# A graph network layer on one core: another order of the end, 28 row tiles instead of 26, and four row addresses with one register load

## The chip, the cores and the metric

The kernel runs on one core of one Trainium2 chip. A core has TensorE (PE: matmuls, with its weight loads shown as PEld), VectorE (DVE), ScalarE (ACT), GpSimd (POOL) and SyncE (SP), which compute or issue in their own order and wait for each other by semaphores. The metric is device time in microseconds (us), the median of several runs.

## The reference

There are 6250 nodes with 128 features, and 206,250 edges sorted by receiver. For each edge, two small networks give a weight vector of 128; the query of the receiver, the key of the sender and this weight are multiplied, summed over each of 8 heads, scaled, and multiply the sender's value. The results are summed by receiver, added to the node features, and normalized by row.

```python
w_ij = silu(edge_feats @ rad_W1 + rad_b1) @ rad_W2 + rad_b2
w_ij = w_ij + (silu(chi_scalar @ sph_W1 + sph_b1) @ sph_W2 + sph_b2)
q_i = (node_feats @ Wq).reshape(-1, 8, 16)[receivers]
k_j = (node_feats @ Wk).reshape(-1, 8, 16)[senders]
alpha = (q_i * w_ij * k_j).sum(axis=-1) / sqrt(16) * cutoffs[:, None]
v_j = (node_feats @ Wv)[senders].reshape(-1, 8, 16)
out = segment_sum(alpha[..., None] * v_j, receivers) / 16
x = layernorm(node_feats + out.reshape(-1, 128))
```

## The kernel before

A tile is 128 edges, one per partition. Four tiles are a quad (512 edges), four quads a group. There are 403 quads in 101 groups; the last group, 100, has three. Inside a group the quads are taken in the order 0, 2, 1, 3; `order` is the list of all quads in that order, and a place in it is called a position.

First the kernel makes a table `kv_tab` in device memory with key and value of every node. Quads at the first ten positions get their sender rows from x instead. For every later quad, POOL gathers four tiles of `kv_tab` rows by sender index (`gathers`, issued 14 positions ahead, at line 127 of the helper `gather`), with 16 buffers. Receivers are sorted, so the receivers of a quad lie in a window of 32 nodes and those of a group in a window of 128; one-hot tables turn queries into rows per edge (`hotT`, `one_hots_T`) and sum messages by receiver (`hot`, `one_hots`).

**Row tiles.** At 26 positions, spread over positions 20 to 392, the last tile of the quad is not gathered by POOL (`row_quads`). SP copies its 128 rows instead, each with a DMA of 1 KB whose source address stands in a register (`load_rows`, lines 150 to 168). It does so in four parts, at four slots before the quad's turn: one register load of 32 addresses from `at_i` (line 163) and 32 DMAs (line 167). The last part comes 8 positions before the quad, so the last of all at position 384. `multiply` and `messages` take such a quad in two instructions, one for three tiles and one for the row tile (`kv_parts`).

**The main loop** (lines 685 to 744) goes over groups g and four slots; the order of each engine is the order of the calls. In a slot, TensorE does the first layers for the quad two ahead (`first_layers`), the queries (`q_at_edges`) and the second layers (`weigh`) for the quad one ahead; ScalarE does the silus; VectorE does `multiply` (query by key, line 526) for the quad one ahead, then `scores` (lines 534, 536, 538) and `messages` (line 551) for the current quad. Messages of group g - 1 are summed in the slots of group g (`sum_quads`). Then `part_sums`, `sum_group` and `place` bring a group's sums to its 128 rows together with what the group before it left (`tot`).

SP's own work in the loop, in this order: in slot 0 `load_x` (the 128 rows of x for group g + 3: a register load of the address from `gb_i`, line 234, and a DMA, line 237); in slot 2 `load_feats` (group g + 3, line 178) and `load_rel` (the receivers `relb` for group g + 2, line 189); in every slot one `write_rows` (one group's rows of out, line 647, if any are ready), and `load_rows`. `load_x` and `load_feats` wait for a mark of TensorE, so that SP does not run ahead. VectorE reads `relb` in slot 1 of the group before (`one_hots_T`, line 218).

`statistics` (slot 3) adds x to a group's sums and takes mean and variance (`moments`, lines 613 to 616); every fourth group, four groups are normalized (`roots`, line 621, and `normalize`, lines 629 to 635).

**The end** (lines 745 to 799) is written out for the last three quads, called a, b and c, all of group 100. Their sums go straight to 128 rows (`sum_wide`, line 578). Quad c is taken in two halves, each with multiply, scores, messages and sums of its own, and groups 97, 98 and 99 are normalized one by one between these; group 100 follows, and its rows are the last write (line 799).

Of the kernel before, what the change touches and what calls it, by code (L numbers as in the profile page):

```python
# [44 lines left out]
ROW_BYTES = 2 * D * 4  # L45
XQ = 10
RING = 16
ROW_TILES = 26
ROW_FIRST = 20
ROW_LAST = 392  # L50
ROW_LEAD = 8
ROW_UNIT = 32
CHECK = 20
XL = 3
NEIGHBORS = 16.0
EPS = 1e-5
SCALE = 1.0 / (math.sqrt(HD) * NEIGHBORS)
# [3 lines left out]
def gnn_kernel(ctx, tc, x, src, dst, weight, edges, rad_W1, rad_b1, rad_W2, rad_b2,  # L61
# [169 lines left out]

    def load_x(g, mark=None):

        r_of[g] = nc.values_load(gb_i[:1, g:g + 1], engines=(SP,), min_val=0, max_val=(N - P) * D * 4,
                                 skip_runtime_bounds_check_because="the table is clamped to it")
        x_of[g] = gp.tile([P, D], F32, name="x", bufs=XL + 4)
        o = nc.sync.dma_start(x_of[g].bitcast(U8), rows_from(x, r_of[g]))
        if mark is not None:
            tc.add_manual_dep(o.ins, mark.ins.name, WAIT, reason="one signal of TensorE a quad")
# [226 lines left out]
    with tc.tile_pool(name="ps", bufs=1, space=PSUM) as pp:  # L466
# [55 lines left out]
        def multiply(q, mark=None, t=slice(0, QT)):  # L522
            if t.start == 0:
                kq_of[q] = quad_of("kq", 3)
            for u, kv in kv_parts(q, t):
                o = nc.vector.tensor_tensor(kq_of[q][:, u, :], pq_of[q][:, u, :], kv[:, :, :D],  # L526
                                            op=OP.mult)
                if mark is not None:
                    after(o, mark)
# [28 lines left out]
        def sum_quads(g, t, j=None):  # L558

            if g not in po_of:  # L560
                po_of[g] = pp.tile([P, D], F32, name="po")
            for j in range(NQ) if j is None else (j,):
                o = nc.tensor.matmul(po_of[g][j * W:(j + 1) * W, :], hot_of[g][:, j * QT + t, :],  # L563
                                     msg_of[g * NQ + j][:, t, :], start=(t == 0), stop=(t == QT - 1))
            return o
# [73 lines left out]
        def statistics(g):  # L639
            moments(g, tot_of[g])  # L640
            if g < NG - LB and first_of(g + 1) > g:
                normalize(first_of(g), g + 1, roots(first_of(g), g + 1))
# [42 lines left out]
        for g in range(NG - 1):  # L685
            for slot, j in enumerate((0, 2, 1, 3)):
                q = g * NQ + j
                i = g * NQ + slot
                turned, past, old = None, mark, marks
                if slot == 0 and g == CHECK + len(checks) + 1:  # L690
                    verdict()
                if slot == 0:
                    turned = turn_q(g + 1, pp.tile([P, EQ], F32, name="pq", bufs=2))
                if slot == 1 and 2 <= g:
                    turned = sum_group(g - 2)
                if slot == 2:
                    turned = make_q(g + 1, pp.tile([P, EQ], F32, name="pq", bufs=2))
                if 1 <= g:
                    for t in ((), (0, 1), (2,), (3,))[slot]:
                        mark = sum_quads(g - 1, t)  # L700
                first_layers(order[i + 2])
                mark = q_at_edges(order[i + 1])
                marks = weigh(order[i + 1])
                silus(order[i + 2], mark, marks)
                if turned:
                    turned()
                if 1 <= g and slot == 3:
                    part_sums(g - 1)
                if i + AHEAD < len(order):
                    gathers(order[i + AHEAD], old[-QT:])  # L710
                multiply(order[i + 1], mark)
                messages(q, scores(q, marks=marks), marks=marks)
                if slot == 0:
                    if g + XL < NG:
                        load_x(g + XL, past)
                if slot == 2:
                    if g + 3 < NG:
                        load_feats(g + 3, past)
                    if g + 2 < NG:
                        load_rel(g + 2)  # L720
                if slot == 1:
                    one_hots_T(g + 1)
                    if g + 2 < NG:
                        pick(g + 2)
                    if 1 <= g:
                        place(g - 1)
                write_rows()
                load_rows(i)
                if slot == 3:
                    if 2 <= g:  # L730
                        statistics(g - 2)
                    if g + 1 < NG - 1:
                        one_hots(g + 1)
                    if CHECK <= g < CHECK + len(checks):
                        checks[g - CHECK]()
                if g == NG - 3 and slot in (0, 2):
                    wide_one_hots(order[slot // 2 - 3])
                if g == NG - 2 and slot == 0:
                    wide_one_hots(order[-1])
                    n = nc.values_load(general, min_val=0, max_val=1)  # L740
                if g == NG - 2 and slot == 2:
                    place(NG - 1)
                if g == NG - 2 and slot == 3:
                    place(g)
        g, (a, b, c) = NG - 1, order[-3:]
        halves = (slice(0, QT // 2), slice(QT // 2, QT))
# [1 line left out]
        mark = q_at_edges(b)  # L748
        marks = weigh(b)
        turned = sum_group(g - 2)  # L750
        for t in range(QT // 2):
            sum_quads(g - 1, t)
        silus(c, mark, marks)
        sd = roots(g - 3, g - 2)
        turned()
        multiply(b, mark)
        messages(a, scores(a, marks=marks), marks=marks)
        normalize(g - 3, g - 2, sd)
        write_rows()

        mark = q_at_edges(c)
        marks = weigh(c)
        for t in range(QT // 2, QT):
            sum_quads(g - 1, t)
        po_of[g] = pp.tile([P, EQ], F32, name="ph", bufs=2)[:, :D]
        for t in range(QT):
            sum_wide(a, t, start=(t == 0))
        part_sums(g - 1)
        turned = sum_group(g - 1)
        messages(b, scores(b, marks=marks), marks=marks)  # L770
        moments(g - 2, tot_of[g - 2])
        sd = roots(g - 2, g - 1)
        turned()
        for t in range(QT):
            sum_wide(b, t)
        nc.tensor.matmul(po_of[g], to_of[g][:, 1, :], tot_of[g - 1], start=False, stop=False)

        multiply(c, mark, halves[0])
        messages(c, scores(c, halves[0]), halves[0])
        for t in range(QT // 2):  # L780
            sum_wide(c, t)
        normalize(g - 2, g - 1, sd)
        write_rows()
        moments(g - 1, tot_of[g - 1])
        sd = roots(g - 1, g)
        multiply(c, mark, halves[1])
        messages(c, scores(c, halves[1]), halves[1])
        for t in range(QT // 2, QT):
            sum_wide(c, t, stop=(t == QT - 1))
        normalize(g - 1, g, sd)  # L790
        write_rows()
        moments(g, po_of[g])
        sd = roots(g, g + 1)
        rs = gp.tile([P, LB], F32, name="rs")
# [163 lines left out]
```

## Time and profile before

| | us |
|---|---|
| median of 3 runs | 2006.75 |
| range of the runs | 2006.64 to 2006.97 |
| the profiled execution | 2007.43 |
| its span, first to last instruction | 2005.3 |
| PE busy | 1806.6 |
| DVE busy | 1468.5 |
| POOL busy | 1502.9 |
| ACT busy | 718.5 |

A row of instructions names line, engine, operation, tiles and count; behind the bar stand busy time, mean ns of one, and idle time before them with what ended it. A row of the order of time gives start, duration, engine and line, and in brackets how long the engine stood idle before it and what released it. A row of waits names who waited for whom: total us, times, longest. SPq is the queue of SP's issues; register loads and DMA issues do not count as busy time. A row of a stretch gives its bounds and length, then busy us (count) of PE, PEld, DVE, ACT and POOL, the granted clock of TensorE, the share of the DMA engines and GB/s; for the instructions of one line alone only its engine stands there.

### The profile page before, as it was taken

Reading aid. Unit: us, or ns where it says so; the run is one execution under the profiler, and the core shown is the slowest. Engines: PE = TensorE matmul, PEld = TensorE weight load, DVE = VectorE, ACT = ScalarE, POOL = GpSimd, SP = SyncE. Lnnn points to the kernel's source line nnn. Section 1 sums busy time; section 2 is a strip of 40 time slices with the busy share of each in tenths; the row PEclk is TensorE's granted clock in tenths of the full one; section 3 lists DMA queues with packets and bytes.
Section 4 is the critical chain, followed back from the end, with each engine's and each line's share of the span. In section 5 each row is a group of like instructions: output and inputs, shape, how many; then the busy total and the mean of one; then the engine's idle time right before and its main releaser. Section 6 shows DMA issues by size and latency. Waiting matters only on the chain.

```text
span 2005.3 us, 51075 instructions
## 1 busy us (share of the span) xinstructions
PE 1806.6 (90%) x16012; PEld 1521.8 (76%) x16012; DVE 1468.5 (73%) x3087; ACT 718.5 (36%) x1426; POOL 1502.9 (75%) x1594
## 2 busy tenths in 40 slices
PE   9999999989899988989998899898988999888897
PEld 7788777867777767778877777777777777777776
DVE  6688787858787767777777676776767767767677
ACT  3244344424343333333333333342433333333333
POOL 7777777777777777777777777777777777777775
PEclk9899989988988988988888889898889888898898
DMA  8545555545555555555555555554455455455453
GB/s 313 158 141 153 149 150 152 157 142 153 154 144 152 155 144 153 154 144 151 155 145 153 147 147 152 144 156 140 141 155 154 143 150 156 142 151 144 139 154 86
DMA packets 146834, 304.50 MB, mean 152 GB/s; under 512 B 36940, under 2 KB 80060, under 8 KB 146556
## 3 DMA queue, kind: packets, MB, share of 16 engines
q0 software_dynamic: 75488, 205.36, 36.7%
q1 hardware_dynamic: 69568, 95.42, 14.6%
q8 instruction: 128, 2.10, 0.4%
q14 instruction: 150, 1.23, 0.2%
q10 hardware_dynamic: 1500, 0.40, 0.1%
HBM read 287.58 MB, written 13.46 MB: 150 GB/s over the span
## 4 chain that ended last, share of the span: by engine, by line
PE 61%; DMA 16%; DVE 9%; issue 5%; ACT 4%; POOL 3%; SPq 1%; DVEq 0%; POOLq 0%; ACTq 0%
PE pw L517 31%; DMA kv<-kv_tab,src_i 12%; PE pq L481 11%; PE ph L472 8%; PE po L563 4%; DVE kq L526 3%; DMA relb<-rel_lin 3%; PE pw L512 3%; POOL msg L127 2%; DVE kq L534 2%; ACT L502 2%; ACT y L635 1%; DVE side L536 1%; PE pq L212 1%; POOL kv L127 1%
## 5 line engine op out<-in xcount | busy, mean ns | idle before, releaser
L127 POOL DMA_INDIRECT kv<-kv_tab,src_i x1546 | 1463.0, 946 | 471.3 <-PE pw L517 182.9
L502 ACT ACTIVATE act<-ph,b 128x512 f32<-128x512 f32 x806 | 517.5, 685 | 1134.8 <-PE pq L481 1093.5
L517 PE MATMUL pw<-w,act 128*128 128x128 f32 x6448 | 914.8, 301 | 0.0
L517 PEld LDWEIGHTS pw<-w,act 128*128 128x128 f32 x6448 | 833.6, 209 | 105.8 <-issue 94.8
L481 PE MATMUL pq<-q,hotT 32*128 32x128 f32 x3224 | 505.5, 300 | 65.9 <-DVE hotT L218 43.0
L472 PE MATMUL ph<-feats,w 32*128 32x512 f32 x1612 | 502.3, 680 | 19.8 <-ACT act L502 19.0
L481 PEld LDWEIGHTS pq<-q,hotT 32*128 32x128 f32 x3224 | 424.8, 201 | 95.3 <-issue 57.7
L526 DVE TENSOR_TENSOR kq<-pq,kv 128x512 f32<-128x512 f32 (+1 forms) x404 | 273.8, 678 | 276.6 <-DMA kv<-kv_tab,src_i 122.2
L536 DVE TENSOR_REDUCE side<-kq 128x32 f32<-128x512 f32 x404 | 280.1, 693 | 42.8 <-DVE kq L534 0.9
L551 DVE TENSOR_TENSOR msg<-kv,side 128x512 f32<-128x512 f32 (+1 forms) x404 | 273.9, 678 | 42.9 <-DVE side L538 0.5
L534 DVE TENSOR_TENSOR kq<-pw,kq 128x512 f32<-128x512 f32 x404 | 274.5, 680 | 0.1
L472 PEld LDWEIGHTS ph<-feats,w 32*128 32x128 f32 x1612 | 136.8, 193 | 105.6 <-issue 60.5
L512 PE MATMUL pw<-brow,onesb 3*128 3x512 bf16 x403 | 162.5, 403 | 7.6 <-DVE kq L534 7.6
L563 PE MATMUL po<-msg,hot 128*32 128x128 f32 x3200 | 158.1, 295 | 0.0
L218 DVE TENSOR_TENSOR hotT<-relb,side 128x512 f32<-128x512 bf16 x101 | 68.9, 682 | 88.7 <-DMA relb<-rel_lin 88.7
L538 DVE TENSOR_TENSOR side<-side,scale 128x32 f32<-128x32 f32 x404 | 80.6, 200 | 42.6 <-DVE side L536 0.9
L597 PE MATMUL pq<-part,to 128*128 128x128 f32 x200 | 44.7, 307 | 68.9 <-DVE kq L526 46.7
L563 PEld LDWEIGHTS po<-msg,hot 128*32 128x32 f32 x3200 | 72.6, 113 | 39.6 <-issue 7.3
L597 PEld LDWEIGHTS pq<-part,to 128*128 128x128 f32 x200 | 31.8, 200 | 76.9 <-issue 43.9
L223 DVE TENSOR_TENSOR hot<-rel,side 128x512 f32<-128x512 f32 x100 | 66.2, 662 | 0.0
L212 PE MATMUL pq<-wq,xT 128*128 128x128 f32 x200 | 45.9, 316 | 18.6 <-DVE kq L526 18.5
L212 PEld LDWEIGHTS pq<-wq,xT 128*128 128x128 f32 x200 | 35.5, 222 | 21.8 <-DVE kq L526 21.4
(114 smaller groups left out, 849.6 us busy)
## 6 DMA issues: line engine op xcount, KB each, us to landing
wide<-kv_tab SPq DMA_DIRECT2D x3328, 1.0 KB
feats<-in_edges SPq DMA_DIRECT2D x101, 512.0 KB
kv<-kv_tab,src_i POOLq DMA_INDIRECT x1546
relb<-rel_lin SPq DMA_DIRECT2D x101, 128.0 KB
x<-in_x SPq DMA_DIRECT2D x101, 64.0 KB
out<-y SPq DMA_DIRECT2D x101, 64.0 KB
kv_tab<-kv SPq DMA_DIRECT2D x12, 512.0 KB
act<-in_x SPq DMA_DIRECT2D x12, 256.0 KB
```

Source lines behind the costliest of these rows:

```text
L127: return nc.gpsimd.indirect_dma_start(out=o, out_offset=None, in_=table, in_offset=bass.IndirectOffsetOnAxis(ap=index, axis=0))
L212: nc.tensor.matmul(pt[:n, :D], xT_of[g][:, :n], wq, start=True, stop=True)
L472: return nc.tensor.matmul(act_of[q, i], w1[r0:r0 + R, :], feats_of[g][r0:r0 + R, c0:c0 + EQ], start=True, stop=True)
L481: o = nc.tensor.matmul(pq_of[q][:, t, :], hotT_of[g][b, t * P:(t + 1) * P], q_of[g][b, :], start=True, stop=True)
L502: o = nc.scalar.activation(act, act_of[q, i], AF.Silu, bias=b1[:, i:i + 1])
L512: nc.tensor.matmul(pw, onesb, brow.rearrange("p t d -> p (t d)"), start=True, stop=False)
L517: o = nc.tensor.matmul(pw[:, t, :], act_of[q, i][:, t * P:(t + 1) * P], w2[:, i, :], start=False, stop=(t == QT - 1 and i == 1))
L526: o = nc.vector.tensor_tensor(kq_of[q][:, u, :], pq_of[q][:, u, :], kv[:, :, :D], op=OP.mult)
L534: nc.vector.tensor_tensor(m, pw_of[q][:, t, :], m, op=OP.mult)
L536: o = nc.vector.tensor_reduce(alpha, m.rearrange("p t (h e) -> p t h e", e=HD), AX.X, OP.add)
L551: o = nc.vector.tensor_tensor(msg_of[q][:, u, :].rearrange("p t (h e) -> p t h e", e=HD), kv[:, :, D:].rearrange("p t (h e) -> p t h e", e ...
L563: o = nc.tensor.matmul(po_of[g][j * W:(j + 1) * W, :], hot_of[g][:, j * QT + t, :], msg_of[g * NQ + j][:, t, :], start=(t == 0), stop=(t = ...
```

## The change

Three things change.

- `ROW_TILES` is 28 instead of 26, over the same positions, so SP copies two more tiles, and POOL issues two gathers fewer (1544 instead of 1546 of `kv`).
- `load_x` loads the addresses of up to four groups with one register load: group 0 alone, then 1 to 4, 5 to 8 and so on, instead of one load for each group. SP has 26 instead of 101 such loads. The DMAs of x stay where they were.
- The end: in group 99 `statistics(97)` and both `place` move from slot 3 to slot 2. Behind the loop, the scores and messages of a come ahead of the multiply of b; all 16 sums of group 99 stand together, and its `part_sums` and `sum_group` come earlier; groups 98 and 99 get their moments together, one `roots` and one `normalize`, and their two writes are issued together; quad c is multiplied and scored whole, and only its messages and sums go in halves. The marks of TensorE that scores and messages waited for are left out in the end.

```diff
-ROW_TILES = 26
+ROW_TILES = 28
...
+XB = 4
...
     def load_x(g, mark=None):
 
-        r_of[g] = nc.values_load(gb_i[:1, g:g + 1], engines=(SP,), min_val=0, max_val=(N - P) * D * 4,
-                                 skip_runtime_bounds_check_because="the table is clamped to it")
+        if g not in r_of:
+            n = min(XB, NG - g) if g else 1
+            _, at = nc.values_load_multi_w_load_instructions(
+                gb_i[:1, g:g + n], engines=(SP,), min_val=0, max_val=(N - P) * D * 4,
+                skip_runtime_bounds_check_because="the table is clamped to it")
+            r_of.update(zip(range(g, g + n), at))
...
-                if slot == 3:
+                if slot == (3 if g < NG - 2 else 2):
                     if 2 <= g:
                         statistics(g - 2)
+                if slot == 3:
                     if g + 1 < NG - 1:
                         one_hots(g + 1)
...
                 if g == NG - 2 and slot == 2:
                     place(NG - 1)
-                if g == NG - 2 and slot == 3:
                     place(g)
...
         turned = sum_group(g - 2)
-        for t in range(QT // 2):
+        for t in range(QT):
             sum_quads(g - 1, t)
         silus(c, mark, marks)
         sd = roots(g - 3, g - 2)
         turned()
+        part_sums(g - 1)
+        messages(a, scores(a))
         multiply(b, mark)
-        messages(a, scores(a, marks=marks), marks=marks)
         normalize(g - 3, g - 2, sd)
         write_rows()
 
         mark = q_at_edges(c)
+        turned = sum_group(g - 1)
         marks = weigh(c)
-        for t in range(QT // 2, QT):
-            sum_quads(g - 1, t)
+        turned()
         po_of[g] = pp.tile([P, EQ], F32, name="ph", bufs=2)[:, :D]
         for t in range(QT):
             sum_wide(a, t, start=(t == 0))
-        part_sums(g - 1)
-        turned = sum_group(g - 1)
-        messages(b, scores(b, marks=marks), marks=marks)
-        moments(g - 2, tot_of[g - 2])
-        sd = roots(g - 2, g - 1)
-        turned()
+        nc.tensor.matmul(po_of[g], to_of[g][:, 1, :], tot_of[g - 1], start=False, stop=False)
+        messages(b, scores(b))
         for t in range(QT):
             sum_wide(b, t)
-        nc.tensor.matmul(po_of[g], to_of[g][:, 1, :], tot_of[g - 1], start=False, stop=False)
-
-        multiply(c, mark, halves[0])
-        messages(c, scores(c, halves[0]), halves[0])
-        for t in range(QT // 2):
-            sum_wide(c, t)
-        normalize(g - 2, g - 1, sd)
-        write_rows()
+        moments(g - 2, tot_of[g - 2])
         moments(g - 1, tot_of[g - 1])
-        sd = roots(g - 1, g)
-        multiply(c, mark, halves[1])
-        messages(c, scores(c, halves[1]), halves[1])
-        for t in range(QT // 2, QT):
-            sum_wide(c, t, stop=(t == QT - 1))
-        normalize(g - 1, g, sd)
-        write_rows()
+        sd = roots(g - 2, g)
+        multiply(c, mark)
+        normalize(g - 2, g, sd)
+        write_rows(2)
+        alpha = scores(c)
+        for h in halves:
+            messages(c, alpha[:, h], h)
+            for t in range(h.start, h.stop):
+                sum_wide(c, t, stop=(t == QT - 1))
         moments(g, po_of[g])
```

## The prediction

> **What bounds the kernel now.** I read the groups of instructions first, then POOL's order of time, then SP's, then what VectorE waits for. All is set against the profiled execution: span 2005.3 us, 2007.43 us in all, 0.68 us above the median of 2006.75 us.
>
> ```profile
> span 2005.3 us, 51075 instructions
> PE 1806.6 (90%) x16012; PEld 1521.8 (76%) x16012; DVE 1468.5 (73%) x3087; ACT 718.5 (36%) x1426; POOL 1502.9 (75%) x1594
> ...
> L127 POOL DMA_INDIRECT kv<-kv_tab,src_i x1546 | 1463.0, 946 | 471.3 <-PE pw L517 182.9
> ...
> 54.26 0.95 POOL L127 DMA_INDIRECT kv<-kv_tab,src_i  x1 [0.30 <-DVE brow L337]
> 1987.24 0.95 POOL L127 DMA_INDIRECT kv<-kv_tab,src_i  x1 [0.30 <-issue]
> DVE kq L526 <- DMA kv<-kv_tab,src_i: 122.2, 65, 5.3
> DVE hotT L218 <- DMA relb<-rel_lin: 88.7, 18, 11.1
> ...
> L526 DVE TENSOR_TENSOR kq<-pq,wide 128x128 f32<-128x128 f32 x26 | 7.3, 281 | 0.0
> ```
>
> POOL's 75% busy share hides that it is full: 1545 steps from the first to the last gather of kv take 1932.98 us, 1.2511 us each, 0.95 of work and 0.30 that precedes every gather, whoever is named. So a group of four quads (16 gathers, 20.02 us) less the gathers that SP replaces, one per row tile, is POOL's pace: with 26 row tiles over 372 quads (one in 14.31) 20.02 - 1.2511 x 4 / 14.31 = 19.67 us a group.
>
> VectorE waits for two things: gathered kv, which is POOL's pace, and relb, which SP loads. SP next:
>
> ```profile
> 438.71 0.35 SPq L237 DMA_DIRECT2D x<-in_x  x1
> 441.13 10.35 SPq L167 DMA_DIRECT2D wide<-kv_tab  x32
> 451.57 0.37 SPq L178 DMA_DIRECT2D feats<-in_edges  x1
> 452.03 0.56 SPq L189 DMA_DIRECT2D relb<-rel_lin  x1
> 453.62 0.35 SPq L237 DMA_DIRECT2D x<-in_x  x1
> 456.01 11.15 SPq L167 DMA_DIRECT2D wide<-kv_tab  x32
> L163 SPq TENSOR_LOAD <-at_i x104: 1869/2104/2488, 123.7 to 1892.0; - x104
> L234 SPq TENSOR_LOAD <-gb_i x101: 267/554/1089, 25.1 to 1913.9; - x101
> L189 SPq EVENT_SEMAPHORE  x28: 17/17/17, 247.4 to 760.0; - x28
> SPq L647 <- DMA out<-y: 40.0, 13, 4.6
> SPq L178 <- PE pw L517: 4.6, 12, 0.7
> ```
>
> There is no room between SP's issues: a burst of 32 row copies (10.4 to 11.2 us) with its register load (2.1 us) costs about 13.0 us, and the loads of feats, relb and x follow at once. One relb is loaded per group; the 28 from 247.4 to 760.0 us make 27 periods of 18.99 us. In that stretch SP waited 4.6 us for TensorE's marks and 40.0 us for earlier writes of out to land, so it was not held back by the consumers: 18.99 us is SP's own pace. It is only 0.68 us faster than POOL's 19.67.
>
> ```profile
> 253.04 0.69 DVE L218 TENSOR_TENSOR hotT<-relb,side 128x512 f32<-128x512 bf16 x1 [10.79 <-DMA relb<-rel_lin]
> 254.36 0.68 DVE L526 TENSOR_TENSOR kq<-pq,kv 128x512 f32<-128x512 f32 x1
> 917.88 0.69 DVE L218 TENSOR_TENSOR hotT<-relb,side 128x512 f32<-128x512 bf16 x1 [3.51 <-DMA relb<-rel_lin]
> 919.20 0.68 DVE L526 TENSOR_TENSOR kq<-pq,kv 128x512 f32<-128x512 f32 x1
> 1982.24 0.95 POOL L127 DMA_INDIRECT kv<-kv_tab,src_i  x1 [0.30 <-issue]
> 1985.60 0.69 DVE L526 TENSOR_TENSOR kq<-pq,kv 128x512 f32<-128x512 f32 x1 [0.75 <-DMA kv<-kv_tab,src_i]
> ```
>
> The last two rows give the landing: 3.3 us after the start of a quad's last gather. The multiply at 254.36 is of the 44th quad, which needs gather 135 (the first ten quads have no gathers of kv, 34 x 4 less one row tile); by then POOL had begun (254.36 - 54.26) / 1.2511 = 160. So the consumers lagged POOL by 25 x 1.25 - 3.3 = 28 us there. At 919.20 (184th quad, gather 685 of 691 begun) it is 4 us, and no wait for relb comes later. The lag fell 24 us in 35 groups, 0.69 a group: the difference of the two paces. **So SP binds up to 920 us, POOL after that**, and the end is POOL's.
>
> **The change, part by part.**
>
> Rows of 28 tiles: one tile in 13.29 quads. Two gathers fewer: POOL ends 2.50 us earlier, and its pace is 20.02 - 1.2511 x 4 / 13.29 = 19.64 us. SP gets 16 / 13.29 - 16 / 14.31 = 0.086 bursts a group more, x 13.0 = +1.12 us. VectorE gets four short instructions more (two tiles' multiplies and messages split off), 4 x 0.28 = 1.1 us, hidden by its 27% of idle time; without that cover they would cost as much.
>
> Addresses of four groups with one load: three of four loads of gb_i go. Such a load costs SP at least its 0.55, at most 0.94 (between the end of relb at 452.59 and x at 453.62 lie 1.03 us, less the 0.09 seen between feats and relb); I take 0.70. A load of four registers is not in this trace: its ends are the one-register load (0.55) and the 32-register load (2.10). The line between them gives (2.10 - 0.55) / 31 = 0.05 a register, so 0.15 more than one. Per group -0.53 + 0.04 = -0.49 us. At the upper end of 2.10 it would be -0.14. Moved x loads: their DMAs stay where they were.
>
> The Trainium skill, Runtime: NRT & Kernel Launch, section Instruction fetch mechanics, puts a register load at about 200 ns a register even in bulk. The trace disagrees: 32 registers took 2.10 us, not 6.4. By the Trainium skill's figure a load of four is, as an estimate, 0.6 us dearer than of one, 0.15 us a group instead of 0.04, and the sum below would be 2025 instead of 2015 us.
>
> **SP's pace after: 18.99 + 1.12 - 0.49 = 19.62 us a group, against POOL's 19.64.** The lag of the first 250 us no longer drains. It starts larger too: SP is 0.63 us a group slower over the eight groups since the rows begin, 5 us. Of 28 to 33 us I take 32; 0.02 x 85 groups = 2 us drain by the last row load, quad 384, which leaves 30.
>
> ```profile
> 350.00:400.00 50.00, 9.03 (x13) 1.00 0.53 156
> ```
>
> After quad 384 SP has no rows and the consumers run free. The row counts L536 (one per quad) in a stretch with little waiting: 13 in 50 us, 3.85 us a quad, against POOL's 5.00. Sixteen quads recover 16 x 1.15 - 1.25 (one row tile, quad 392) = 17 us. So 13 us of lag remain at the last group: 13 - 2.5 = **+10.5 us**.
>
> **The order of the end.**
>
> ```profile
> 1985.60:1997.25 11.65, 8.44 (x89) 7.14 (x87) 10.47 (x30) 3.21 (x9) 1.98 (x3) 1.00 0.16 48
> 1983.51 0.31 DVE L613 TENSOR_TENSOR y<-tot,x 128x128 f32<-128x128 f32 x1
> 1984.51 0.34 DVE L587 TENSOR_SCALAR to<-side,rowp 128x128 f32<-128x128 f32 x1
> 1988.10 0.69 DVE L551 TENSOR_TENSOR msg<-kv,side 128x512 f32<-128x512 f32 x1
> 1992.21 0.41 DVE L526 TENSOR_TENSOR kq<-pq,kv 128x256 f32<-128x256 f32 x1
> 1993.86 0.42 DVE L551 TENSOR_TENSOR msg<-kv,side 128x256 f32<-128x256 f32 x1
> 1997.14 0.15 DVE L629 RECIPROCAL rs<-sd 128x1 f32<-128x1 f32 x1
> 1997.33 0.16 DVE L631 SCALAR_TENSOR_TENSOR shift<-mv,rs 128x1 f32<-128x1 f32 x1
> 1999.48 0.35 DVE L798 TENSOR_SCALAR y<-y,mv,rs 128x128 f32<-128x128 f32 x1
> 2000.85 0.34 SPq L799 DMA_DIRECT2D out<-y  x1
> ```
>
> VectorE (10.47 of 11.65 us busy) sets this stretch, so what counts is its chain:
> - The last quad in halves takes 1.65 us from L526 to L551 and 0.42 for L551, twice: 4.14. Whole, it takes 2.50 (1985.60 to 1988.10) and two half messages, 3.34: -0.8.
> - Two groups normalized together: one pair L629, L631 less, -0.3.
> - Statistics and two one-hot tables move one slot earlier (1983.51 to 1984.85, 1.3 us): the same work, ahead of the multiply of the third-last quad. The 0.75 us of waiting behind it goes: with 13 us of lag kv has long landed, and next late is VectorE itself.
> - The third-last quad's scores now go ahead of the second-last's multiply, so TensorE, which needs that pq buffer back, starts the last quad's q about 1 us later. Its weighting takes about 3 us more and is needed after two moments and a multiply, some 2 us of cover; without it up to 1 us. All sums of group 99 now stand together on TensorE; their messages are done by then: 0.
> - SP issues the last write 1.0 us after y is done (1999.83 to 2000.85), behind the landing of the write before. Now the two writes before it are issued together; the second waits for the first to land (nothing but the last write is queued behind), yet both start earlier. The 1.0 shrinks by 0 to 1.0; I take 0.6.
>
> Sum: -0.8 - 0.3 - 0.75 - 0.6 = **-2.5 us** (0 to -3).
>
> Total: +10.5 - 2.5 = +8, so 2006.75 + 8 = **2014.8 us**.
>
> **The rivals.**
> - *POOL stays the bound: faster.* From a pace of SP 0.15 us a group lower (19.47) on, 13 us more drain by quad 384 and no lag is left at the end. What could give it: the 40.0 us of waits for writes of out, 1.5 us a group, shrink by a tenth because more bursts stand between two writes; or a gb_i load is worth 0.9. Against it: the balance of the paces is measured over 27 groups. It gives 2006.75 - 2.5 - 2.5 = 2001.8 us.
> - *Partly drained*: SP lower by 0.03 to 0.12 us a group, lag 3 to 10 us at the end: 2001.8 plus that, 2005 to 2012 us.
> - *The load of four is dear*: half way between its two ends, 1.33 us, it adds 0.19 a group instead of 0.04; SP's pace is 19.77, the lag grows by 0.13 x 85 = 11 us instead of losing 2: 2028 us. At the upper end (SP at 19.97) it is 2045. For it speaks only that no such load was seen; against it that 31 more registers cost 1.55 us. The Trainium skill, Runtime: NRT & Kernel Launch, section Instruction fetch mechanics, is on this rival's side.
> - *The new end gains nothing*: 2017 us.
>
> **How the numbers follow.** The two paces differ by less than I can read either, so the cases lie close. Forecast (2010 to 2019, its own range; the new end without gain lies in it) 0.42; POOL stays the bound 0.27; partly drained 0.18; dear load or beyond 2019 otherwise 0.13. Within 0.2% (4 us, about what a measurement of this kernel can tell from none) lies most of the partly drained case: same 0.17; faster 0.27; slower 0.56. The range goes from the first rival, 2001, to the dear load, 2028, and leaves out about 1 in 10, the load's upper end with it.
>
> **What would show it.** Right: relb loads of SP about 19.6 us apart, waits of hotT for relb of 200 to 350 us instead of 88.7 and going on past 1000 us up to about 1900, fewer waits for kv, the last gather at about 1984.7 and more than 10 us before the last multiply. The four-register load reads 0.6 to 0.8 us. In the end, no wait for kv, VectorE without gaps. Wrong: waits for relb that stop half way, kv waits to the end; a span near 2000.5 then says that SP kept up.

## The result and the profile after

The changed kernel takes 2028.51 us (median of 6 runs, 2024.77 to 2033.96); the kernel before took 2006.70 us beside it (6 runs, 2006.17 to 2007.16). The ratio is 1.0108, with a 95% interval of 1.0097 to 1.0118: slower by 1.1%, 21.8 us. The profiled execution took 2025.42 us.

The first lines are the span, the shares of the chain that ended last (those of the kernel before stand in the last line), and the two waits that the prediction followed (total us, times, longest).

```profile
span 2023.3 us, 51510 instructions
...
PE 48%; SPq 14%; DMA 12%; DVE 12%; issue 7%; ACT 4%; POOL 2%; DVEq 0%; ACTq 0%; POOLq 0%
...
DVE hotT L219 <- DMA relb<-rel_lin: 282.6, 43, 14.6
DVE kq L531 <- DMA kv<-kv_tab,src_i: 22.3, 18, 2.9
...
PE 61%; DMA 16%; DVE 9%; issue 5%; ACT 4%; POOL 3%; SPq 1%; DVEq 0%; POOLq 0%; ACTq 0%
```

SP's share of the chain has gone from 1% to 14%. The waits of hotT for relb went from 88.7 us (18 times) to 282.6 (43), those for gathered kv from 122.2 to 22.3. The limit has moved from POOL to SP. SP's own rows (count, duration min/median/max in ns, first and last start) and its order of time near the end follow. Below them stand POOL's last gather, its last one for the third-last quad and some rows of VectorE; the last two rows are the same gather and multiply in the kernel before. Lines 163, 167, 178, 189, 218, 237, 526, 647 and 799 of the kernel before are 164, 168, 179, 190, 219, 242, 531, 652 and 796 here; the register load of addresses is line 237.

```profile
L237 SPq TENSOR_LOAD <-gb_i x26: 1088/1165/1411, 24.1 to 1903.8; - x26
L190 SPq DMA_DIRECT2D relb<-rel_lin x73: 539/562/607, 262.7 to 1679.6; - x73
...
1926.78 10.89 SPq L168 DMA_DIRECT2D wide<-kv_tab  x32
1937.76 0.37 SPq L179 DMA_DIRECT2D feats<-in_edges  x1
1938.23 0.58 SPq L190 DMA_DIRECT2D relb<-rel_lin  x1
...
2010.22 6.71 SPq L652 DMA_DIRECT2D out<-y  x3
2019.52 0.34 SPq L796 DMA_DIRECT2D out<-y  x1
```

```profile
1974.59 0.95 POOL L128 DMA_INDIRECT kv<-kv_tab,src_i  x1 [0.30 <-issue]
1984.60 1.03 POOL L128 DMA_INDIRECT kv<-kv_tab,src_i  x1 [0.30 <-PE pw L522]
...
1943.75 0.69 DVE L219 TENSOR_TENSOR hotT<-relb,side 128x512 f32<-128x512 bf16 x1 [12.21 <-DMA relb<-rel_lin]
...
2003.34 0.68 DVE L531 TENSOR_TENSOR kq<-pq,kv 128x512 f32<-128x512 f32 x1
...
2019.14 0.35 DVE L795 TENSOR_SCALAR y<-y,mv,rs 128x128 f32<-128x128 f32 x1
...
1977.25 0.94 POOL L127 DMA_INDIRECT kv<-kv_tab,src_i  x1 [0.30 <-issue]
...
1980.41 0.69 DVE L526 TENSOR_TENSOR kq<-pq,kv 128x512 f32<-128x512 f32 x1 [0.16 <-PE pq L481]
```

POOL starts its last gather 2.64 us earlier than before (1987.24), near the forecast. But the third-last multiply, which in the kernel before starts as its last gather lands (1980.41; 1977.25 and the 3.3 us of landing), now starts 25.5 us after that (2003.34 less 1974.59 and the 3.3 us). This distance is the lag of the multiplies behind POOL, and it is meant by "lag" below. The stretch from the start of the third-last multiply to the end of the span is shorter: from 1980.4 to 2005.3 us before, from 2003.34 to 2023.3 after, 4.9 us less. So 25.5 - 2.6 - 4.9 = 18.0 us, which is the difference of the two profiled executions (2025.42 - 2007.43).

### The profile page after: what moved, and what is told of

Same layout as the page of the kernel before. It is cut to its first block, busy times and chain, and to the rows that moved or that the text cites. A ratio compares the mean times of both kernels' runs of the same rounds, so it can differ in the third digit from the quotient of the medians.

```text
span 2023.3 us, 51510 instructions
## 1 busy us (share of the span) xinstructions
PE 1772.8 (88%) x16012; PEld 1494.3 (74%) x16012; DVE 1462.9 (72%) x3087; ACT 717.2 (35%) x1425; POOL 1501.1 (74%) x1592
## 3 DMA queue, kind: packets, MB, share of 16 engines
q14 instruction: 154, 1.25, 0.2%
## 4 chain that ended last, share of the span: by engine, by line
PE 48%; SPq 14%; DMA 12%; DVE 12%; issue 7%; ACT 4%; POOL 2%; DVEq 0%; ACTq 0%; POOLq 0%
PE pw L522 25%; SPq L168 10%; PE pq L486 9%; DMA relb<-rel_lin 7%; PE ph L477 6%; DMA kv<-kv_tab,src_i 3%; PE po L568 3%; SPq L164 3%; DVE kq L531 3%; PE pw L517 2%; DVE kq L539 2%; DVE side L541 2%; POOL msg L128 2%; DMA out<-y 2%; ACT L507 1%
## 5 line engine op out<-in xcount | busy, mean ns | idle before, releaser
L522 PE MATMUL pw<-w,act 128*128 128x128 f32 x6448 | 902.2, 298 | 0.0
L522 PEld LDWEIGHTS pw<-w,act 128*128 128x128 f32 x6448 | 821.6, 207 | 108.0 <-issue 96.8
L486 PE MATMUL pq<-q,hotT 32*128 32x128 f32 x3224 | 497.1, 296 | 172.4 <-DVE hotT L219 170.5
L486 PEld LDWEIGHTS pq<-q,hotT 32*128 32x128 f32 x3224 | 418.4, 199 | 201.4 <-issue 197.8
L477 PE MATMUL ph<-feats,w 32*128 32x512 f32 x1612 | 485.4, 659 | 24.9 <-ACT act L507 24.2
L219 DVE TENSOR_TENSOR hotT<-relb,side 128x512 f32<-128x512 bf16 x101 | 69.1, 684 | 282.6 <-DMA relb<-rel_lin 282.6
L568 PE MATMUL po<-msg,hot 128*32 128x128 f32 x3200 | 151.1, 285 | 0.0
L517 PEld LDWEIGHTS <-onesb 3*128 3x128 bf16 x403 | 37.4, 93 | 16.4 <-DVE kq L539 14.9
L128 POOL DMA_INDIRECT msg<-in_x,src_x x40 | 38.9, 974 | 13.3 <-issue 11.9
```

The costliest lines, as they stand in the source:

```text
L128: return nc.gpsimd.indirect_dma_start(out=o, out_offset=None, in_=table, in_offset=bass.IndirectOffsetOnAxis(ap=index, axis=0))
L477: return nc.tensor.matmul(act_of[q, i], w1[r0:r0 + R, :], feats_of[g][r0:r0 + R, c0:c0 + EQ], start=True, stop=True)
L486: o = nc.tensor.matmul(pq_of[q][:, t, :], hotT_of[g][b, t * P:(t + 1) * P], q_of[g][b, :], start=True, stop=True)
L517: nc.tensor.matmul(pw, onesb, brow.rearrange("p t d -> p (t d)"), start=True, stop=False)
L522: o = nc.tensor.matmul(pw[:, t, :], act_of[q, i][:, t * P:(t + 1) * P], w2[:, i, :], start=False, stop=(t == QT - 1 and i == 1))
```

## The experiments

The theory was that SP and POOL run at nearly the same pace, and that every microsecond a group on SP decides which of them sets the end. The rivals: the new end costs the time; relb is late because its transfer is slow, not because it is issued late.

The runs are of two kinds. In one, the kernel before takes 2005 to 2008 us, as in the result; in the other 2612 to 2670 us, at a granted TensorE clock of 0.80 to 0.83 instead of 0.90 to 0.92. The chip's number does not tell them apart: number 12 stands at runs of both kinds (`end_only_e` and `end_only_f`). In the second kind VectorE waits above all for TensorE, and SP's pace can't be seen. The runs of that kind come last.

**The new end alone** (`end_only_f`; rows of 26 tiles, one address a load).

```diff
-ROW_TILES = 28
+ROW_TILES = 26
...
-XB = 4
+XB = 1
```

> Rows of 26 tiles and one address a load, as before; only the new order of the end is kept, where POOL's pace sets the end (the kernel before at 2006 us). The kernel with 27 tiles gained 4.9 us, 1.25 of it by POOL's one gather less; so the end should be worth 3.6 us, 2002.9 us, between the forecast 2.5 (2004) and the 4.9 (2001.5) by which the changed kernel's tail got shorter; hotT's waits for relb as before, about 90 us. If the new order costs time, it is slower than 2007 us.

Measured: 2002.79 us against 2006.91, ratio 0.9980 (0.9971 to 0.9989), 4.1 us faster.

```profile
DVE kq L531 <- DMA kv<-kv_tab,src_i: 135.6, 80, 4.9
DVE hotT L219 <- DMA relb<-rel_lin: 69.1, 18, 10.6
```

The two waits are those of the kernel before in kind: much kv, little relb, POOL's limit. The end is a gain where POOL sets the limit, so the slowdown comes from the other two parts.

**28 tiles by rows alone** (`rows_only_f`; one address a load, old end).

```diff
-ROW_TILES = 26
+ROW_TILES = 28
```

> 28 tiles by rows, one address a load, the old end, where SP's and POOL's paces decide (the kernel before at 2006 us). My theory: SP's pace is 18.99 + 1.12 = 20.11 us a group against POOL's 19.64; the lag grows by 0.47 x 85 = 40 us from about 30 at 250 us, and little is recovered after the last row load. 2040 to 2070 us, with waits of hotT for relb beyond 400 us in sum. If 28 tiles were no load for SP, this kernel gains POOL's 2.5 us: 2004 us.

Measured: 2042.75 us against 2006.16, ratio 1.0184 (1.0164 to 1.0204), 36.6 us slower. The lines are the waits, and SP's loads of relb for groups 12 to 84.

```profile
DVE hotT L218 <- DMA relb<-rel_lin: 293.4, 44, 14.9
DVE kq L526 <- DMA kv<-kv_tab,src_i: 25.7, 17, 2.9
...
L189 SPq DMA_DIRECT2D relb<-rel_lin x73: 542/567/627, 262.0 to 1692.5; - x73
```

The 73 loads make 72 periods of (1692.5 - 262.0) / 72 = 19.87 us, against POOL's 19.64. In the first 36 of them, where SP binds in the kernel before too, the pace was 20.14 us (262.0 to 987.0) with 44 bursts; before it was 18.88 (263.0 to 942.8) with 40. So four more bursts cost 45 us, 11.3 each, where 13.0 were taken: this term of the forecast stands. The time lies at the lower edge of the expectation and the wait for relb far below the 400 us; by the trace the lag grew from 30 us (position 40) to about 41 (the middle value from position 150 on), not by 40. The time came out all the same, because nothing was recovered at the end: the lag was 36.9 us at position 380 and 39.1 at 401.

**27 tiles** (`tiles27_c`; the changed kernel otherwise).

```diff
-ROW_TILES = 28
+ROW_TILES = 27
```

> The changed kernel with 27 tiles by rows instead of 28, where SP's and POOL's paces decide (the kernel before at 2006 us). My theory: one tile less takes 0.043 x 13.0 = 0.56 us a group off SP's pace and adds 0.015 to POOL's, so the lag drains at about 0.55 us a group and is gone after some 50 groups; the end is POOL's, 1.25 us earlier than before, and the new end brings its 3 to 5 us: 2000 to 2003 us. If the lag is made by something other than SP's rows, 27 tiles move the time by a few us only: 2020 to 2027 us.

Measured: 2001.66 us (2000.98 to 2001.93) against 2006.54, ratio 0.9977 (0.9967 to 0.9987).

```profile
DVE hotT L219 <- DMA relb<-rel_lin: 133.3, 29, 12.4
DVE kq L531 <- DMA kv<-kv_tab,src_i: 104.1, 65, 4.1
...
L190 SPq DMA_DIRECT2D relb<-rel_lin x73: 535/562/959, 261.0 to 1649.2; - x73
```

One tile fewer on SP is worth 27 us: over the same 72 periods SP comes every 19.28 us instead of 19.68. That is below POOL's pace of about 19.65, so the lag drains (18.6 us at position 100, 2.2 at 183) and POOL sets the end. The kv waits are back. The time lies in the expected range: 4.1 us of the end and one gather of 1.25 make 5.35, and 4.9 were measured. This version is faster than both kernels; its ratio and that of `end_only_f` are the same within their intervals.

**What a register load costs by its count** (`load_cost`; in six row tiles of the kernel before, each burst loads its addresses in six parts).

```diff
+SPLIT = (1, 2, 3, 4, 6, 16)
...
-            _, rows = nc.values_load_multi_w_load_instructions(
-                at_i[k:k + 1, e:e + ROW_UNIT], engines=(SP,), min_val=0,
+            for n in SPLIT if k in SPLIT_TILES else (ROW_UNIT,):
+                _, rows = nc.values_load_multi_w_load_instructions(
+                    at_i[k:k + 1, e:e + n], engines=(SP,), min_val=0,
...
```

> The kernel before, but in six of its 26 row tiles (the 17th to the 22nd) each burst of 32 rows loads its addresses in six parts, of 1, 2, 3, 4, 6 and 16 registers, each followed by its row copies. It gives the duration of a register load on SP by count, 24 times each. My prediction's line from 0.55 us (one) to 2.10 us (32), 0.05 us a register, would give 0.60, 0.65, 0.70, 0.80 and 1.30 us for 2, 3, 4, 6 and 16. A price of 0.2 us a register from the first on, which the load of four in the changed kernel speaks for (1.165 us), gives 0.75, 0.96, 1.17, 1.57 us for 2, 3, 4 and 6, and must bend before 32: 16 at 1.6 to 2.1 us. SP pays some 4 us a burst for the five more loads, so the time is above that of the kernel before.

The rows below are single loads of one line, of 2, 3, 4, 6, 16 and 32 registers in this order (duration in ns, three times the same value for one instruction).

```profile
L166 SPq TENSOR_LOAD <-at_i x1: 739/739/739, 1720.3 to 1720.3; - x1
L166 SPq TENSOR_LOAD <-at_i x1: 940/940/940, 1721.8 to 1721.8; - x1
L166 SPq TENSOR_LOAD <-at_i x1: 1146/1146/1146, 1723.9 to 1723.9; - x1
L166 SPq TENSOR_LOAD <-at_i x1: 1595/1595/1595, 1726.8 to 1726.8; - x1
L166 SPq TENSOR_LOAD <-at_i x1: 1266/1266/1266, 1760.7 to 1760.7; - x1
L166 SPq TENSOR_LOAD <-at_i x1: 2037/2037/2037, 1622.3 to 1622.3; - x1
```

The medians of 24 each are 0.71, 0.94, 1.15, 1.57 and 1.27 us for 2, 3, 4, 6 and 16, and 2.07 for 32. So there are two branches: 0.2 us a register for small counts, and, by the two points there are, 0.05 a register (on 0.47) for 16 and 32. Six cost more than sixteen. My line between one register and 32 joined points of two different branches. The Trainium skill, Runtime: NRT & Kernel Launch, section Instruction fetch mechanics, gives about 200 ns a register, for loads in bulk too: with that, the steps between the loads of two to six agree (0.21 to 0.23 us a register), and the loads of 16 and 32 don't. Whether the count decides or the address (the loads of 16 and 32 begin at multiples of 16 values, the others don't) these runs don't separate. This run is of the second kind (2664.31 us against 2652.09, one run), so its time tells nothing more.

**Eight addresses a load** (`xb8`).

```diff
-XB = 4
+XB = 8
```

> The changed kernel with the addresses of eight groups with one register load. The loads of 2, 3, 4 and 6 registers took 0.71, 0.94, 1.15 and 1.57 us, but that of 16 only 1.27 and that of 32 2.07: a load of eight is either on the dear branch (0.2 us a register, 1.98 us) or on the cheap one (0.47 + 0.05 a register, 0.87 us). Dear: (1.98 + 0.19) / 8 = 0.27 us a group against 0.34 with four, 0.07 less, 6 us less lag by the last row load. Cheap: (0.87 + 0.19) / 8 = 0.13, 0.21 less, 18 us less lag, which is most of it. Where SP's pace decides, the time falls by 4 to 6 us or by 15 to 18 us against the changed kernel's 2028.5; where TensorE sets the pace throughout, it stays.

Measured: 2016.67 us (2011.08 to 2019.99) against 2006.39, ratio 1.0056 (1.0040 to 1.0073): 12 us less than the changed kernel.

```profile
L237 SPq TENSOR_LOAD <-gb_i x11: 1142/1952/2214, 335.4 to 1888.9; - x11
L190 SPq DMA_DIRECT2D relb<-rel_lin x73: 539/560/607, 256.9 to 1665.0; - x73
```

The load of eight is on the dear branch, 1.95 us, and the gain is twice the 4 to 6 us that it accounts for. SP's pace over the 72 periods is 19.56 us, 0.12 less than with four, and not 0.07; the trace is of the fastest of the four runs. The other half of the gain stays open; the runs of these kernels scatter by 4 us and more to either side.

**relb one group earlier** (`rel_early`; SP's work is the same).

```diff
-        relb_of[g] = gp.tile([P, EQ], BF16, name="relb")
+        relb_of[g] = gp.tile([P, EQ], BF16, name="relb", bufs=3)
...
+        load_rel(2)
...
-                    if g + 2 < NG:
-                        load_rel(g + 2)
+                    if g + 3 < NG:
+                        load_rel(g + 3)
```

> The changed kernel with relb in three buffers instead of two, its load issued by SP one group (20 us) earlier in the order; SP's work is the same. My theory: consumers lag POOL by 25 us at the end only because relb, issued three quads before it is needed, is SP's tightest load; a group earlier gives it 20 us more room, so the lag at the end falls from 25 to 4 to 8 us, hotT's waits for relb from 283 to under 100 us, and the time from 2028 to 2003 to 2010 us. If another of SP's loads (rows, x, feats) is as tight, the wait moves to it and the time stays above 2020.

Measured: 2012.44 us (2002.04 to 2014.78) against 2006.40, ratio 1.0029 (1.0016 to 1.0041): 16 us less than the changed kernel, for the same instructions in another order. Of its fastest run, which is the profiled one:

```profile
DVE hotT L219 <- DMA relb<-rel_lin: 121.9, 36, 10.8
PE pq L204 <- DMA x<-in_x: 95.9, 22, 10.1
PE ph L477 <- DMA feats<-in_edges: 87.3, 23, 10.5
```

The waits for relb fall by 160 us, but x and feats, which were hardly ever late before (2.6 us in one wait for x), now are. So SP is late with everything, and relb only had the least room. The traces also speak against a slow transfer: from the issue of a late relb on SP to the hotT that waited for it there are 5.1 to 6.3 us in the kernel before and 4.6 to 5.9 in the changed one (waits over 2 us). The median time lies between what the two expectations said: most of the lag hung on relb, the rest on the next loads in the queue. In the profiled run 3.4 us of lag are left at position 400; the runs that took ten more were not profiled.

**relb from ScalarE's queue** (`rel_act`; of the second kind).

```diff
-        nc.sync.dma_start(relb_of[g], r[:, None, :].to_broadcast([NQ, W, EQ]))
+        nc.scalar.dma_start(relb_of[g], r[:, None, :].to_broadcast([NQ, W, EQ]))
```

> The changed kernel, with the load of relb issued from ScalarE's queue instead of SP's. My theory: relb is late only because SP issues it behind its rows; off SP it lands in time, hotT's waits for it fall below 50 us, SP's pace falls by one DMA issue (about 0.56 us) a group, and POOL sets the end: 2000 to 2003 us. If relb is late because the transfer itself is slow beside more small copies, the waits stay and so does the time, within 5 us of 2028. If ScalarE, which issues it, becomes late by it (101 issues of about 0.56 us among 36% busy time), the time lies between.

Measured: 2977.21 us against 2659.04, ratio 1.1224 (1.1181 to 1.1267). None of the expectations came out.

```profile
SPq L168 <- DMA relb<-rel_lin: 193.4, 38, 10.5
...
PE pq L204 <- DMA x<-in_x: 331.6, 52, 13.0
```

By the semaphores of the trace, SP's row copies now wait for relb, which they neither read nor write: 38 waits, up to 10.5 us (in the kernel before 17 waits, 8.4 us in all). What in the program couples them was not followed up. Off SP's queue, relb held up SP more than on it, and TensorE waited for x as well, 331.6 us against 1.0 in `rows_only_b` beside it.

**The runs of the second kind.** The parts were run there as well, with the edits above; `loads_only` is the kernel before with loads of four addresses alone:

```diff
+XB = 4
...
-        r_of[g] = nc.values_load(gb_i[:1, g:g + 1], engines=(SP,), min_val=0, max_val=(N - P) * D * 4,
-                                 skip_runtime_bounds_check_because="the table is clamped to it")
+        if g not in r_of:
+            n = min(XB, NG - g) if g else 1
+            _, at = nc.values_load_multi_w_load_instructions(
+                gb_i[:1, g:g + n], engines=(SP,), min_val=0, max_val=(N - P) * D * 4,
...
+            r_of.update(zip(range(g, g + n), at))
```

The expectations follow in the order of the runs. First, four kernels together:

> Rows of 26 tiles and one address a load, as before; only the new order of the end is kept. If the slowdown comes from SP's late relb (my theory), this kernel keeps POOL as its bound and gains at the end alone: between the forecast 2.5 us and the 4.9 us by which the changed kernel's tail got shorter, so 2002 to 2004 us, with 18 or so waits of hotT for relb (about 90 us) as before. If the new order itself costs the time (the rival), it is slower than 2007 us.

> Rows of 26 tiles and the old end; only the address loads of four are new. My theory: SP saves 0.70 - 1.36 / 4 = 0.36 us a group, its pace goes from 18.99 to 18.63 us, the lag of the first 250 us is drained at 28 / (19.67 - 18.63) = 27 groups later, some 150 to 200 us earlier than before, and the end is POOL's as before: 2006 to 2007.5 us. hotT's waits for relb fall below the 88.7 us of before, to 50 to 80. The rival, that loads of four registers cost SP more than four of one, gives more waits for relb than before and a time above 2007.5 us if they outweigh POOL.

> 28 tiles by rows, one address a load, the old end. My theory: SP's pace is 18.99 + 1.12 = 20.11 us a group against POOL's 19.64; the lag grows by 0.47 x 85 = 40 us from about 30 at 250 us, and little is recovered after the last row load. 2040 to 2070 us, with waits of hotT for relb beyond 400 us in sum. If 28 tiles were no load for SP and the time of the changed kernel came from the other two parts, this kernel gains POOL's 2.5 us: 2004 us.

> The changed kernel with 27 tiles by rows instead of 28. My theory, that SP's and POOL's paces stand at balance in the changed kernel and decide: one tile less takes 0.043 x 13.0 = 0.56 us a group off SP and adds 0.015 to POOL, so the lag drains at about 0.55 us a group and is gone after some 50 groups; the end is POOL's, 1.25 us earlier than before, and the new end brings its 3 to 5 us: 2000 to 2003 us. If the lag is made by something other than SP's rows (the new end, the load of four), 27 tiles move the time by a few us only: 2020 to 2027 us.

Then, beside the run of relb from ScalarE's queue:

> The kernel of rows_only, where SP's and POOL's paces decide (the kernel before at 2006 us). My theory: SP's pace is 18.99 + 1.12 = 20.11 us a group against POOL's 19.64; the lag grows by 0.47 x 85 = 40 us from about 30 at 250 us, and little is recovered after the last row load. 2040 to 2070 us, with waits of hotT for relb beyond 400 us in sum. If 28 tiles were no load for SP, this kernel gains POOL's 2.5 us: 2004 us.

> The kernel of end_only, where POOL's pace sets the end (the kernel before at 2006 us). My theory: SP and POOL are untouched, and the time falls by what the new end is worth, between the forecast 2.5 and the 4.9 us by which the changed kernel's tail got shorter: 2001.5 to 2004 us, with 18 or so waits of hotT for relb, about 90 us, as before. If the new order itself is what costs the changed kernel its time, this one is slower than 2007 us.

> The kernel of tiles27, where SP's and POOL's paces decide. My theory: one tile less takes 0.043 x 13.0 = 0.56 us a group off SP's pace and adds 0.015 to POOL's, so the lag drains at about 0.55 us a group and is gone after some 50 groups; the end is POOL's, 1.25 us earlier than before, and the new end brings its 3 to 5 us: 2000 to 2003 us. If the lag is made by something other than SP's rows, 27 tiles move the time by a few us only: 2020 to 2027 us.

And 28 tiles three times more, the new end once more:

> 28 tiles by rows, one address a load, the old end, where SP's and POOL's paces decide (the kernel before at 2006 us). My theory: SP's pace is 18.99 + 1.12 = 20.11 us a group against POOL's 19.64; the lag grows by 0.47 x 85 = 40 us from about 30 at 250 us, and little is recovered after the last row load. 2040 to 2070 us, with waits of hotT for relb beyond 400 us in sum. If 28 tiles were no load for SP, this kernel gains POOL's 2.5 us: 2004 us.

> 28 tiles by rows, one address a load, the old end, where SP's and POOL's paces decide (the kernel before at 2006 us). My theory: SP's pace is 18.99 + 1.12 = 20.11 us a group against POOL's 19.64; the lag grows by 0.47 x 85 = 40 us from about 30 at 250 us, and little is recovered after the last row load. 2040 to 2070 us, with waits of hotT for relb beyond 400 us in sum. If 28 tiles were no load for SP, this kernel gains POOL's 2.5 us: 2004 us.

> 28 tiles by rows, one address a load, the old end, where SP's and POOL's paces decide (the kernel before at 2006 us). My theory: SP's pace is 18.99 + 1.12 = 20.11 us a group against POOL's 19.64; the lag grows by 0.47 x 85 = 40 us from about 30 at 250 us, and little is recovered after the last row load. 2040 to 2070 us, with waits of hotT for relb beyond 400 us in sum. If 28 tiles were no load for SP, this kernel gains POOL's 2.5 us: 2004 us.

> Rows of 26 tiles and one address a load, as before; only the new order of the end is kept, where POOL's pace sets the end (the kernel before at 2006 us). SP and POOL are untouched; the time falls by what the new end is worth, between the forecast 2.5 and the 4.9 us by which the changed kernel's tail got shorter: 2001.5 to 2004 us, with 18 or so waits of hotT for relb, about 90 us, as before. If the new order itself costs the changed kernel its time, this one is slower than 2007 us.

| kernel | ratios to the kernel before, 95% interval |
|---|---|
| loads of four alone | 0.9999 (0.9986 to 1.0013) |
| 28 tiles alone | first 0.9999 (0.9987 to 1.0011); b 0.9992 (0.9978 to 1.0007); c 1.0014 (1.0001 to 1.0027); d 1.0015 (0.9994 to 1.0035); e 1.0002 (0.9984 to 1.0019) |
| 27 tiles with loads of four and the new end | first 0.9991 (0.9980 to 1.0003); b 0.9987 (0.9974 to 0.9999) |
| new end alone | first 0.9979 (0.9965 to 0.9993); b 0.9990 (0.9971 to 1.0009); e 0.9989 (0.9973 to 1.0005) |

The times that the first four expectations named were all missed, since they took the kernel before to be at 2006 us; the later ones state that condition. About SP nothing could be shown here: neither its gains nor its losses reach the end. The new end is ahead by 3 to 5 us each time (2651.81 - 2646.71, 2659.04 - 2655.73, 2621.30 - 2618.24), about the 4.1 us of `end_only_f`, but only the first of the three is clear of noise.

The page of one of them (28 tiles alone, run d) with its waits:

```profile
span 2625.2 us, 51600 instructions
...
PE 2129.9 (81%) x16012; PEld 1767.8 (67%) x16012; DVE 1475.1 (56%) x3093; ACT 726.3 (28%) x1426; POOL 1502.7 (57%) x1592
...
DVE kq L526 <- PE pw L517: 527.7, 210, 7.4
...
DVE kq L526 <- DMA kv<-kv_tab,src_i: 1.8, 1, 1.8
```

VectorE waits for TensorE, 1.8 us in all for kv and never for relb, so neither POOL (busy 57%) nor SP holds it up. Why TensorE, busy 81%, is late stays open. Another 287.7 us of its waits end with something that the profile does not name. The same 28 tiles that cost 1.8% elsewhere cost 0.15% at most by the five ratios.

Loads of four alone were not run where SP binds; their worth there follows by difference: the changed kernel's +21.8 us, less +36.6 for the tiles and -4.1 for the end, leaves -10.7 us. That takes the parts to add up, and the traces say that the end is worth less there: from the multiply at position 390 to the end of the span `rows_only_f` takes 68.7 us with the old end, the changed kernel 67.2 with the new one, 1.6 less and not 4.1. With that, and the 13.6 us by which the loads shorten SP's 72 periods (below), 36.6 - 13.6 - 1.6 = 21.4 us, near the measured 21.8.

## Why the prediction was right and where it was wrong

The direction and the mechanism were right: SP's pace comes up to POOL's, relb is late to the end, and the gains of POOL and of the end are smaller than the lag. The size was not: 2014.8 us forecast, 2028.51 measured (+8 forecast, +21.8 measured), half a microsecond beyond the range.

- *SP binds early, POOL late.* Shown. One tile more or less on SP moves the limit from one to the other: kv waits of 104 us with 27 tiles, 22 with 28.
- *POOL ends 2.50 us earlier.* 2.64 us.
- *Two more tiles: +1.12 us a group on SP.* 1.26 by `rows_only_f`, with four bursts more in 36 groups, where the forecast has three.
- *Loads of four: -0.49 us a group.* Mis-sized. A load of four takes 1.17 us, not 0.6 to 0.8; the cause is the two branches above. Against `rows_only_f`, with the same bursts (44 in the first 36 periods, 43 in the last), SP's 72 periods shrank from 1430.5 to 1416.9 us: 0.19 a group. The rule of the Trainium skill that I set aside was right for this count.
- *SP's pace 19.62 against POOL's 19.64, lag about 30 us.* 19.68 by the 73 loads of relb quoted above, and a lag between 24 and 35 us at four of five positions from 60 to 350, 30 in the middle. But 19.68 is an average: SP's pace was 19.93 over the first 36 periods and 19.43 over the last 36. So the sum of the terms held on average, though the load's term didn't, and that it held so closely is luck. Part of what made up for it: by the traces, SP's writes of out, with their waits for the write before, took 1.92 us a group in the first 36 periods and 1.83 in the last, and 2.03 in the first 36 of the kernel before.
- *17 us are recovered after position 384.* **This is the step that failed**, and it is nearly all of the miss, 12.5 of 13.7 us: the forecast left 13 us of lag at the end, the trace shows 25.5. The lag was 21.5 us at position 384, 30.9 at 387, 27.0 at 390 and 25.4 at 400, so nothing of it was recovered behind 384, and 5 us behind 387. It failed twice. First, the consumers don't run free from 384. SP itself was late there: its last burst was issued from 1926.78 to 1937.67 us, relb behind it at 1938.23, and hotT waited for that relb 12.21 us, until 1943.75 (position 387). Second, the pace of 3.85 us a quad was read in a plain stretch in the middle, at a granted clock of 1.00, and the last quads carry more, at 0.89. The last two rows are the whole of both stretches, the kernel before first:

```profile
1956.11 0.69 DVE L531 TENSOR_TENSOR kq<-pq,kv 128x512 f32<-128x512 f32 x1 [0.36 <-PE pq L486]
1960.53 0.68 DVE L531 TENSOR_TENSOR kq<-pq,kv 128x512 f32<-128x512 f32 x1
1963.62 0.55 DVE L531 TENSOR_TENSOR kq<-pq,kv 128x384 f32<-128x384 f32 x1
...
1968.25 0.69 DVE L531 TENSOR_TENSOR kq<-pq,kv 128x512 f32<-128x512 f32 x1
1972.08 0.69 DVE L579 TENSOR_TENSOR wide<-d,side 128x512 f32<-128x512 f32 x1
1972.68 0.69 DVE L531 TENSOR_TENSOR kq<-pq,kv 128x512 f32<-128x512 f32 x1
...
2003.34 0.68 DVE L531 TENSOR_TENSOR kq<-pq,kv 128x512 f32<-128x512 f32 x1
...
DVE kq L531 <- PE pq L486: 3.9, 3, 1.8
...
350.00:400.00 50.00, 48.08 (x500) 41.03 (x498) 44.24 (x92) 21.05 (x42) 37.83 (x40) 1.00 0.53 156
...
1956.10:2003.30 47.20, 44.70 (x395) 37.47 (x396) 39.52 (x88) 19.87 (x39) 22.53 (x24) 0.89 0.32 94
```

  Ten quads from position 390 to 400 take 47.2 us, 4.72 each, with no wait for kv or relb in them. A quad with nothing beside it takes 3.09 (1960.53 to 1963.62); one with hotT and its group's tables 4.42 (1956.11 to 1960.53), one with a wide one-hot table for the end 4.43 (1968.25 to 1972.68). There are three of these wide tables in the last groups, and three waits for TensorE's queries, 3.9 us in all. So of the 0.87 us a quad above 3.85, 0.39 is waiting for TensorE and 0.48 is VectorE's own chain, which is busy 39.52 of the 47.2 us. TensorE is busier still, 44.70 us, and its clock is lower than in the stretch of the forecast; how much of the waiting comes from the clock these runs don't separate. At 4.72 against POOL's 4.9 the ten quads give back less than 2 us. `rows_only_f` agrees: its lag was not recovered either.
- *The end: -2.5 us.* 4.1 by `end_only_f`, beyond the end of its range (3). One term is seen: the last write starts at 2019.52, with y done at 2019.49, so all of the 1.0 us of waiting went, where 0.6 was taken. The remaining 1.2 us were not taken apart. In the changed kernel, with its lag, the new end is worth less (see above).
- *The rival of the dear load.* Its price (1.33 us for a load of four) was nearer to the measured 1.17 than mine, and its time (2028 us) came out. Its mechanism did not: the lag did not grow by 11 us, it merely stayed.

Put together: 2014.8, + 12.5 for the missing recovery, - 2.4 for the last stretch (4.9 us shorter, 2.5 were forecast), is 2024.9; the profiled execution took 2025.42, and the median is 3 us above it.

## What to carry to other kernels

Where two queues run within a few hundredths of the same pace, a part of 1 us a group on either decides tens of microseconds at the end; before more work is moved to the emptier-looking queue, take its pace from the spacing of one of its regular instructions in the stretch where it binds, and leave a margin: 27 tiles won 4.9 us where 28 lost 21.8. A recovery at the end is to be costed from the last groups' own rows, with the extra work and the granted clock that stand there, and from the time at which the late queue has really issued its last piece. Where an operation's price is taken between two measured sizes, allow for a step between them.

## What was unexpected of the hardware

- A register load on SP costs 0.71, 0.94, 1.15, 1.57 and 1.95 us for 2, 3, 4, 6 and 8 registers, but 1.27 for 16 and 2.07 for 32.
- Kernels that SP holds back scatter from run to run (2024.77 to 2033.96, 2002.04 to 2014.78, 2011.08 to 2019.99 and 2040.75 to 2044.92 us); those that POOL holds back scatter less (2000.98 to 2001.93, 2002.41 to 2003.49, 2006.17 to 2007.16).
- The same kernel took 2005 to 2008 us in some runs and 2612 to 2670 in others, once under the same chip number. The granted clock (0.80 to 0.83 against 0.90 to 0.92) goes with it, but is a smaller step than the time; what else slows those runs stays open.
- A relb load issued from ScalarE's queue made SP's unrelated row copies wait up to 10.5 us for it, as the trace's semaphores tell.
